# Four graph layers on one core: unread products in TensorE's idle time, a new order of layer 0, shorter neighbour lists, and a finish from two dot products

## The chip, the cores and the metric

The kernel runs on one core of one Trainium2 chip. A core has five engines with a queue each: TensorE (PE; its weight loads are shown as PEld), VectorE (DVE), ScalarE (ACT), GpSimd (POOL) and SyncE (SP), and DMA engines that move data between the chip's memory (HBM) and the on-chip memory (SBUF). Products land in PSUM[...]. The metric is the device time of one execution in microseconds. Before the change it is 1101.07 us (median of three runs, 1095.69 to 1104.53). The profiled execution, from which all times within the kernel come, took 1025.59 us, of which 1023.6 us lie between its first and last instruction.

## The reference

`x` has 4096 rows of 64 values and `adj` is a 4096 x 4096 matrix of zeros and ones, each one with a chance of 0.000976562, so about four neighbours per row. Four layers follow one another; each normalizes `x` per row, takes the positive part `h`, and adds its result to `x`. Layer 0 is the one that the change touches:

```python
c = 1.0 / r[0] ** 2
x_t = logmap0(x, c)
left = x_t @ w_att[:D, 0]
right = x_t @ w_att[D:, 0]
adj_att = jax.nn.sigmoid(left[:, None] + right[None, :] + b_att[0]) * adj
x_local = logmap(x[:, None, :], x[None, :, :], c)
support_t = jnp.einsum('ij,ijd->id', adj_att, x_local)
return proj(expmap(x, support_t, c), c)
```

So for each pair of neighbours it needs a hyperbolic logarithm (with square roots and logarithms), weights it with an attention value, sums over the neighbours, and maps the sum back. Layers 1 to 3 are products with `adj` (mean of neighbours, two hops with tanh, and a sum over the last 100 neighbours with halving weights).

## The kernel before, in words

Layer 0 (`neighbours`) uses that `adj` is almost empty. It has four kinds of work, for eight blocks of 512 rows:

- **The stream.** `load` brings the transposed adjacency in 64 pieces of 1 MB, three buffers in turn. ScalarE casts each to 8 bits (L781 into SBUF for the first three blocks, L784 and a store to HBM for the rest), for the later layers. TensorE multiplies it with `wpack` (L789), which packs 16 entries of a column into one number; after four pieces ScalarE adds a number that tells the word (`kt`, L795) and TensorE transposes into the key banks (L797).
- **The lists** (`lists`, on VectorE). For each of the 512 rows of a block the largest keys are taken (L819 to L821), taken apart into neighbour numbers (up to L858), and the first four neighbours per row go to `idx`. Rows with more put the rest into a common overflow list, which is packed over the partitions with two small products (`pb` L882, `pc` L903) and gives `ovx`, `own` and `rows_at`.
- **The gathers** (L941, on POOL): 24 indirect DMAs per block fetch rows of a table of 69 values per node (`rows_d`, written once at the beginning), 16 of them after `idx`, 8 after `ovx` and `own`. They land in `es` and `hi`, of which there are two, each for a pair of blocks. So the gathers of pair 2 wait for the product of pair 0, and those of pair 3 for that of pair 1.
- **The sums.** `chunk` forms inner products (L972 to L985), `weights` the weights of a pair of blocks with three ScalarE functions, each with a table load (L1009, L1016, L1032), L1063 scales the rows, `spots` makes the matrices that send overflow rows to their places (L1049), and TensorE sums in float32 (L1069, L1075) into the one bank `v`, from which ScalarE copies (L1080). `finish` (four groups of 8 x 128 rows) maps back and adds to `x` (L1100 to L1178).

The order is written by a planner at build time: it holds a clock, takes steps of these jobs by priority, and adds a cost for each (`yield 1.35`). The result is a fixed queue per engine. Its clock is VectorE's and POOL's alone:

```python
while any(queues.values()):
    now = clock["now"]
    while can_pack() and arrives(packed[0]) <= now + 1.0:
        pack_one()
    hungry = clock["pool"] - now < BACKLOG
    order = ["list", "chunk", "sum", "spot", "finish"] if hungry else ["chunk", "sum", "list", "spot", "finish"]
```

TensorE's and ScalarE's instructions are placed where the job that makes them happens to be recorded. Each engine then works through its queue from the front. Layers 1 to 3 (`layers123`) come behind layer 0 in every queue; most of their time is TensorE's (L1384, L1513, L1526, L1537).

Of the kernel before, what the change touches and what calls it, by code (L numbers as in the profile page):

```python
# [7 lines left out]
F32 = mybir.dt.float32  # L8
BF16 = mybir.dt.bfloat16
# [8 lines left out]
P = 128  # L18
# [32 lines left out]
HOLD, FETCH = -1.0, 1000.0  # L51
STREAM_AT, PACE_MB, PACKED = 7.0, 3.55, 5.0
ROWS_AT, PACE_DMA, LANDED, SUMMED, BACKLOG, SLOW = 46.0, 1.27, 5.0, 6.0, 20.0, 1.1
# [525 lines left out]
def neighbours(ctx, tc, x_in, x, sh, adj_t, adj8, a8, over):  # L579
# [20 lines left out]
    def load(b, v):  # L600
# [17 lines left out]
        noff, pattern=[[2 * N, LB], [0, 16]], base=1 - 127 * NCH, channel_multiplier=0,  # L618
        allow_small_or_imprecise_dtypes=True,
    )  # L620

# [8 lines left out]
    V.tensor_scalar(pr_i, pidx, 15, None, op0=ALU.bitwise_and)  # L630
    V.tensor_scalar(pc_i, pidx, 4, None, op0=ALU.logical_shift_right)
# [8 lines left out]
    V.tensor_scalar(pr_i, pidx, 7, 5, op0=ALU.bitwise_and, op1=ALU.logical_shift_left)  # L640
    V.tensor_scalar(pc_i, pidx, 3, None, op0=ALU.logical_shift_right)
# [3 lines left out]
    io128 = l0.tile([P, P], F32, name="io128")  # L645
    V.tensor_scalar_add(io128, io[:, :P], -1.0)
    before = l0.tile([P, P], BF16, name="before")
    V.tensor_scalar(before, sh.diff, 0.0, None, op0=ALU.is_gt)

# [19 lines left out]
    def inv_root(a, n, name):  # L669

        y = l0e.tile([P, n], F32, tag=f"ir_y{n}", name=f"{name}_y")
        e = l0e.tile([P, n], F32, tag=f"ir_e{n}", name=f"{name}_e")
        S.activation(y, a, AF.Abs_reciprocal_sqrt)
        yield 0.1
        V.tensor_mul(e, y, y)
        yield 0.2
        V.tensor_mul(e, e, a)
        yield 0.2
        V.scalar_tensor_tensor(e, e, -10.0 / 3.0, e, op0=ALU.add, op1=ALU.mult)
        yield 0.2  # L680
        V.scalar_tensor_tensor(y, e, 5.0, y, op0=ALU.add, op1=ALU.mult)
        yield 0.2
        V.tensor_scalar_mul(y, y, 0.375)
        yield 0.2
        return y
# [75 lines left out]

    def row_rest():

        V.tensor_scalar(beta, x2, negc_t, 1.0, op0=ALU.mult, op1=ALU.add)
        V.tensor_scalar_max(clipb, beta, MIN_NORM)


    keys = {}

    def pack(u):  # L770
# [3 lines left out]
        if part == 0:  # L774
            keys[b] = [psum.tile([P, 2, NW], F32, tag="k", bufs=4, name=f"keys{b}_{s}") for s in range(2)]
# [18 lines left out]
        kt = l0w.tile([P, 512], F32, tag="kt", name=f"kt{u}")  # L794
        S.activation(kt, pk, AF.Identity, bias=num[:, part : part + 1])  # L795
        for k in range(LB):
            T.transpose(  # L797
                keys[b][k // 2][:, k % 2, part * P : part * P + P], kt[:, k * P : (k + 1) * P], sh.ident
            )
        yield  # L800


    flags = l0.tile([P, NR, 4], F32, name="flags")
    V.memset(flags, 0.0)
# [4 lines left out]
    turned = [0]  # L809

    def lists(nb):
# [3 lines left out]
        k16 = tile_("k16", [LB, 16])  # L815
        scr = tile_("scr", [NW])
        for k in range(LB):
            kk = keys[nb][k // 2][:, k % 2, :]
# [5 lines left out]
        V.tensor_reduce(flags[:, nb, 0:1], k16[:, :, 15], AX.X, ALU.max)  # L824
        V.tensor_scalar(flags[:, nb, 0:1], flags[:, nb, 0:1], 256.0, None, op0=ALU.is_ge)
        yield 0.3


        ki, wi = tile_("ki", [LB, 16], I32), tile_("wi", [LB, 16], I32)
        wf, vf = tile_("wf", [LB, 16]), tile_("vf", [LB, 16])  # L830
        V.tensor_copy(ki, k16)
        V.tensor_scalar(wi, ki, NW - NCH, 4, op0=ALU.bitwise_and, op1=ALU.logical_shift_left)
        V.tensor_add(wf, wi, noff)
        yield 0.6
        V.tensor_scalar(wi, ki, NCH - 1, None, op0=ALU.bitwise_and)
        V.tensor_add(wf, wf, wi)
        V.tensor_scalar(wi, ki, 8, None, op0=ALU.logical_shift_right)
        V.tensor_copy(vf, wi)
        yield 0.8
        cand = tile_("cand", [LB, 3, 16])  # L840
        for lev in range(3):
            V.tensor_scalar(wi, vf.bitcast(I32), 0x7F800000, None, op0=ALU.bitwise_and)
            V.tensor_sub(vf, vf, wi.bitcast(F32))
            yield 0.4
            V.scalar_tensor_tensor(cand[:, :, lev, :], wi, NCH * 2.0**-23, wf, op0=ALU.mult, op1=ALU.add)
            V.scalar_tensor_tensor(cand[:, :, lev, :], wi, 0.0, cand[:, :, lev, :], op0=ALU.is_gt, op1=ALU.mult)
            yield 0.5
        V.tensor_reduce(flags[:, nb, 1:2], vf, AX.XY, ALU.max)

        j8 = tile_("j8", [LB, 8])  # L850
# [4 lines left out]
        ji = tile_("ji", [LB, NS], I32)  # L855
        V.tensor_copy(ji, j8[:, :, :NS])
        V.tensor_scalar(ji, ji, 2 * N - 1, None, op0=ALU.bitwise_and)
        V.tensor_scalar_min(idx[nb], ji, N)  # L858
        yield 0.6
        yield HOLD  # L860
        gather_slots(nb)
        yield FETCH + PACE_DMA * LB * NS
# [4 lines left out]
        yield 0.8  # L867
        ov, om = tile_("ov", [NV]), tile_("om", [NV])
# [7 lines left out]
        cnt, cnb, at0 = tile_("cnt", [1]), tile_("cnb", [1], BF16), tile_("at0", [1])  # L876
        mv = tile_("mv", [2 * NV + 2], BF16)
        V.tensor_scalar(om, ov, 0.0, None, op0=ALU.is_gt)
        V.tensor_reduce(cnt, om, AX.X, ALU.add)
        V.tensor_copy(cnb, cnt)  # L880
        pb = psum.tile([P, 512], F32, tag="s", bufs=1, name=f"pb{nb}")
        T.matmul(pb[:, :1], before, cnb, start=True, stop=True)  # L882
        V.tensor_copy(mv[:, :NV], ov)
        V.tensor_sub(mv[:, NV : 2 * NV], ov, mv[:, :NV])
        V.tensor_copy(mv[:, 2 * NV + 1 :], p_f)
        V.tensor_copy(flags[:, nb, 2:3], ov[:, NV - 1 : NV])
        yield 1.5

        bi, end = tile_("bi", [1], I32), tile_("end", [1])
        from_, mine = tile_("from", [512], BF16), tile_("mine", [512], BF16)  # L890
        V.tensor_copy(at0, pb[:, :1])
        V.tensor_scalar(from_, io, at0, None, op0=ALU.is_gt)
        V.tensor_add(end, at0, cnt)
        V.scalar_tensor_tensor(mine, io, end, from_, op0=ALU.is_le, op1=ALU.mult)
        yield 1.4
        V.tensor_copy(bi, at0)
        V.tensor_scalar(bi, bi, P - 1, None, op0=ALU.bitwise_and)
        V.tensor_copy(mv[:, 2 * NV : 2 * NV + 1], bi)
        V.tensor_scalar(flags[:, nb, 3:4], end, float(NO * P), 0.0, op0=ALU.subtract, op1=ALU.max)
        pc = psum.tile([P, 512], F32, tag="s", bufs=1, name=f"pc{nb}")  # L900
        pe = pc[:, : NO * (2 * NV + 2)].rearrange("p (c e) -> p c e", c=NO)
        for c in range(NO):
            T.matmul(pe[:, c, :], mine[:, c * P : (c + 1) * P], mv, start=True, stop=True, skip_group_check=True)  # L903
        yield 0.7

        got, ei, ti = tile_("got", [NO, 2]), tile_("ei", [NO], I32), tile_("ti", [NO], I32)
        tf, ef, rw = tile_("tf", [NO]), tile_("ef", [NO]), rows_at[nb]
        its, num2 = tile_("its", [NO, NV]), tile_("num2", [NO, 2, NV])
        V.tensor_copy(got, pe[:, :, 2 * NV :])
        V.tensor_scalar(ti, got[:, :, 0], -1.0, p_f, op0=ALU.mult, op1=ALU.add)  # L910
        V.tensor_scalar(ti, ti, P - 1, None, op0=ALU.bitwise_and)
        V.tensor_copy(tf, ti)
        yield 0.7
        V.tensor_tensor(its, io128[:, None, :NV].to_broadcast([P, NO, NV]), bc(tf, NV), op=ALU.is_equal)
        V.tensor_mul(
            num2, pe[:, :, : 2 * NV].rearrange("p c (t s) -> p c t s", t=2),
            its[:, :, None, :].to_broadcast([P, NO, 2, NV]),
        )
        V.tensor_reduce(tf, num2, AX.XY, ALU.add)
        V.tensor_copy(ei, tf)  # L920
        yield 1.3
        V.tensor_scalar(ti, ei, 2 * N - 1, None, op0=ALU.bitwise_and)
        V.tensor_scalar_min(ovx[nb], ti, N)
        V.tensor_scalar(ti, ei, 13, None, op0=ALU.logical_shift_right)
        V.tensor_scalar(ef, tf, 0.0, None, op0=ALU.is_gt)
        V.scalar_tensor_tensor(rw, got[:, :, 1], float(NCH), ti, op0=ALU.mult, op1=ALU.add)
        V.scalar_tensor_tensor(rw, rw, float(1 + LB * nb), ef, op0=ALU.add, op1=ALU.mult)
        V.tensor_scalar_min(own[nb], rw, float(N))
        yield 1.3
        gather_packed(nb)  # L930
        yield FETCH + PACE_DMA * 2 * NO
        V.scalar_tensor_tensor(rw, ti, float(P), got[:, :, 1], op0=ALU.mult, op1=ALU.add)
        V.scalar_tensor_tensor(rw, rw, 1.0, ef, op0=ALU.add, op1=ALU.mult)
        yield 0.4
# [53 lines left out]
    def weights(se, e_g, x2i, lf, name):  # L988
# [23 lines left out]
        yield 0.6  # L1012

# [3 lines left out]
        yield 0.2  # L1017
        V.tensor_mul(e, y, y)
# [15 lines left out]
        yield 0.2  # L1034
        V.scalar_tensor_tensor(den, den, -1.0, gap, op0=ALU.add, op1=ALU.subtract)
# [7 lines left out]
    vs, spot = {}, {}  # L1043
# [7 lines left out]

    def sums(g, q0, q1):
# [5 lines left out]
        if q0 == 0:  # L1058
            vs[g] = l0w.tile([P, 8, DQ], F32, tag="vs", bufs=4, name=f"vs{g}")
        for q in range(q0, q1):  # L1060
# [4 lines left out]
            bank = psum.tile([P, 512], F32, tag="v", bufs=1, name=f"v{nb}")  # L1065
            pv = bank[:, : LB * DQ]
            slots = es[g][:, q, : LB * NS, :DQ].rearrange("p (k s) e -> p s k e", k=LB)
            for s in range(NS):
                T.matmul(  # L1069
                    pv.rearrange("p (k e) -> p k e", k=LB), sh.ident, slots[:, s], start=(s == 0), stop=False,  # L1070
                    skip_group_check=True,
                )
            for c in range(NO):
                for k in range(LB):
                    T.matmul(  # L1075
# [603 lines left out]
```

## Time and profile before

| | value |
|---|---|
| time, median of 3 | 1101.07 us |
| profiled span | 1023.6 us |
| last adjacency piece packed | from 256.6 us |
| gathers on POOL | 192, from 61.3 to 349.2 us |
| end of layer 0 (last addition to `x`) | 440.1 us |
| first large product of layer 1 | 491.2 us |
| mean granted TensorE clock | 0.807 |

The span in 40 slices of 25.6 us: each digit is the busy share of a slice in tenths, PEclk the granted TensorE clock in tenths of full speed, DMA the share of the DMA engines. The first 17 slices are layer 0.

```profile
PE   3545556555622630017999989998996899999996
DVE  4769775769278548864455531113444345444443
ACT  4666574555301231222111111112222343434342
POOL 0347777676067500000000000000000000000000
PEclk9955559555565765557899999998998899999999
DMA  8699997999011100072000000000000000000000
```

And the groups of gathers, pack products and block sums: line, engine, operation, output and inputs, count, then busy us and mean ns of one, and the idle time of the engine before them with what ended it.

```profile
L789 PE MATMUL pk<-a,wpack 128*128 128x512 bf16 x256 | 111.3, 582 | 97.4 <-DMA a<-in_adj_t 97.4
L941 POOL DMA_INDIRECT es<-rows_d,idx x128 | 128.1, 1001 | 95.3 <-issue 35.0
L1069 PE MATMUL v<-es,ident 128*128 128x260 f32 x64 | 25.8, 571 | 30.1 <-issue 23.1
L1075 PE MATMUL v<-es,spot 128*128 128x65 f32 x256 | 37.8, 318 | 0.0
```

[...] several in a row take less than count times mean.

### The profile page before, as it was taken

The page shows a single profiled execution, that of the slowest core. Times are in us where ns is not written, and L with a number is a line of the kernel's source. Part 1 is how long each engine was busy: PE and PEld are TensorE (multiplying, and loading weights), DVE is VectorE, ACT ScalarE, POOL GpSimd, SP SyncE. Part 2 cuts the span into 40 slices and gives each one's busy share as a digit, 9 for nine tenths or more (in the row PEclk, how much of TensorE's full clock was granted, in tenths as well). Part 3 has the DMA queues.
Part 4 walks back from the last instruction along what each step waited for, and adds up shares of the span by engine and source line. Part 5 has one row for each costly group of instructions (what it writes and reads, how often), then busy time and mean ns, then how long its engine had stood idle before and what let it go on. Part 6 is the DMA issues. An engine that isn't in the chain of part 4 may idle for free.

```text
span 1023.6 us, 14344 instructions
## 1 busy us (share of the span) xinstructions
PE 705.4 (69%) x5602; PEld 532.8 (52%) x5602; DVE 551.8 (54%) x1705; ACT 344.2 (34%) x465; POOL 200.5 (20%) x208
## 2 busy tenths in 40 slices
PE   3545556555622630017999989998996899999996
PEld 1112115211512530017899989998995565656564
DVE  4769775769278548864455531113444345444443
ACT  4666574555301231222111111112222343434342
POOL 0347777676067500000000000000000000000000
PEclk9955559555565765557899999998998899999999
DMA  8699997999011100072000000000000000000000
GB/s 284 235 355 332 373 377 250 379 378 360 13 21 28 19 0 0 0 316 96 1 1 1 2 1 2 1 1 2 2 2 1 1 1 12 1 11 1 11 2 14
DMA packets 49248, 99.49 MB, mean 97 GB/s; under 512 B 6802, under 2 KB 6802, under 8 KB 48274
## 3 DMA queue, kind: packets, MB, share of 16 engines
q1 hardware_dynamic: 35232, 79.70, 21.5%
q10 hardware_dynamic: 7794, 11.98, 3.2%
q0 software_dynamic: 6144, 6.80, 3.1%
q8 instruction: 46, 0.75, 0.3%
q14 instruction: 32, 0.26, 0.1%
HBM read 85.79 MB, written 12.67 MB: 96 GB/s over the span
## 4 chain that ended last, share of the span: by engine, by line
PE 49%; DVE 5%; ACT 3%; issue 1%; ACTq 0%
PE l2b_acc L1384 9%; PE l2a_acc L1384 9%; PE l_acc L1513 8%; PE l_acc L1384 8%; PE cnt L1537 7%; PE cnt L1526 5%; PE l_u L1344 1%; PE l_t L1331 1%; ACT l_h L1333 1%; DVE l_agg L1365 1%; PE l2b_u L1344 0%; PE l_u L1338 0%; DVE l_r L1351 0%; DVE ln_c L1609 0%; DVE ln_c L1615 0%
## 5 line engine op out<-in xcount | busy, mean ns | idle before, releaser
L1384 PEld LDWEIGHTS <-a 128*128 128x128 fp8e4 x3072 | 265.5, 99 | 9.3 <-issue 6.9
L789 PE MATMUL pk<-a,wpack 128*128 128x512 bf16 x256 | 111.3, 582 | 97.4 <-DMA a<-in_adj_t 97.4
L1533 DVE TENSOR_SCALAR wt<-cnt 128x512 int16<-128x512 f32 x128 | 88.5, 692 | 121.0 <-PE cnt L1526 121.0
L941 POOL DMA_INDIRECT es<-rows_d,idx x128 | 128.1, 1001 | 95.3 <-issue 35.0
L1534 ACT ACTIVATE wt<-cnt,low_t 128x512 int16<-128x512 f32 x128 | 87.9, 687 | 134.8 <-PE cnt L1526 134.8
L789 PEld LDWEIGHTS <-wpack 128*128 128x128 bf16 x256 | 33.0, 130 | 159.3 <-issue 144.9
L1513 PE MATMUL l_acc<-y_b,wt 128*128 128x192 bf16 x1024 | 106.7, 247 | 0.0
L1513 PEld LDWEIGHTS <-wt 128*128 128x128 bf16 x1024 | 89.1, 98 | 31.3 <-issue 1.7
L1537 PE MATMUL cnt<-a,fill 128*128 128x512 fp8e4 x248 | 81.2, 382 | 20.3 <-DVE wt L1533 20.0
L1384 PE MATMUL l_acc<-y_a,a 128*128 128x193 bf16 x1024 | 94.9, 253 | 0.0
L784 ACT CAST f<-a 128x2048 fp8e4<-128x2048 f32 x40 | 75.9, 1898 | 48.2 <-DMA a<-in_adj_t 47.1
L1384 PE MATMUL l2b_acc<-y_a,a 128*128 128x192 bf16 x1024 | 89.2, 249 | 3.0 <-DVE y_a L1353 3.0
L1384 PE MATMUL l2a_acc<-y_b,a 128*128 128x192 bf16 x1024 | 88.1, 248 | 3.0 <-DVE y_b L1353 3.0
L1526 PE MATMUL cnt<-a,tri 128*128 128x512 fp8e4 x256 | 77.2, 383 | 0.0
L781 ACT CAST a<-a 128x2048 fp8e4<-128x2048 f32 x24 | 45.3, 1894 | 22.9 <-DMA a<-in_adj_t 18.5
L1069 PE MATMUL v<-es,ident 128*128 128x260 f32 x64 | 25.8, 571 | 30.1 <-issue 23.1
L1526 PEld LDWEIGHTS <-tri 128*128 128x128 bf16 x256 | 24.7, 97 | 37.4 <-issue 22.4
L1639 PE MATMUL po<-one,over 128*1 128x1 f32 x2 | 0.2, 163 | 58.8 <-DVE over L1281 58.8
L1075 PEld LDWEIGHTS v<-es,spot 128*128 128x128 f32 x256 | 38.8, 238 | 1.2
L1537 PEld LDWEIGHTS <-fill 128*128 128x128 bf16 x248 | 24.0, 97 | 28.1 <-issue 21.3
L1075 PE MATMUL v<-es,spot 128*128 128x65 f32 x256 | 37.8, 318 | 0.0
L1365 DVE TENSOR_REDUCE l2a_agg<-l2a_acc 128x128 f32<-128x384 f32 x16 | 8.9, 558 | 51.4 <-PE l2a_acc L1384 51.4
(336 smaller groups left out, 828.6 us busy)
## 6 DMA issues: line engine op xcount, KB each, us to landing
a<-in_adj_t SPq DMA_DIRECT2D x64, 1024.0 KB, 8.3
adj<-f ACTq DMA_DIRECT2D x40, 256.0 KB, 6.4
a<-adj SPq DMA_DIRECT2D x5, 2048.0 KB, 19.5
es<-rows_d,idx POOLq DMA_INDIRECT x128, 5.5
rows_d<-tab ACTq DMA_DIRECT2D x1, 1104.0 KB, 4.8
x<-in_x SPq DMA_DIRECT2D x1, 1024.0 KB
out<-z SPq DMA_DIRECT2D x4, 256.0 KB, 2.1
es<-rows_d,ovx POOLq DMA_INDIRECT x32, 5.4
```

The lines of the kernel that those rows point to most:

```text
L781: S.copy(a8[b][:, 4 * at : 4 * at + 4, :], a, saturate=False)
L784: S.copy(f8, a, saturate=False)
L789: T.matmul(pk, wflat[:, w * P : (w + 1) * P], bits[:, j, :, 1], start=(w == 0), stop=(w == 15),)
L941: G.indirect_dma_start(out=dst, out_offset=None, in_=rows_d, in_offset=bass.IndirectOffsetOnAxis(ap=at, axis=0))
L1069: T.matmul(pv.rearrange("p (k e) -> p k e", k=LB), sh.ident, slots[:, s], start=(s == 0), stop=False, skip_group_check=True,)
L1075: T.matmul(pv[:, k * DQ : (k + 1) * DQ], spot[nb][:, c, k * P : (k + 1) * P], es[g][:, q, LB * NS + c, :DQ], start=False, stop=(c == NO - ...
L1384: T.matmul(acc, a8[n // 4][:, c, n % 4 * P : (n % 4 + 1) * P], y3[:, c, :cols], start=(c == first[0] and k % 2 == 0), stop=(c == last[-1] ...
L1513: T.matmul(accs[k // 2][:, k % 2, : 3 * D], wts[k // 4][:, (k % 4) * P : (k % 4 + 1) * P].bitcast(BF16), y3[:, c, : 3 * D], start=(c == NC ...
L1526: T.matmul(cnt[b], tri, masks[b], start=head_, stop=last, skip_group_check=True)
L1533: V.tensor_scalar(wts[0], cnt[0], -(128.0 - MAX_NEIGH) * UNIT, 0.0, op0=ALU.add, op1=ALU.max)
L1534: S.activation(wts[1], cnt[1], AF.Relu, bias=low_t)
L1537: T.matmul(cnt[b], fill, masks[b], start=False, stop=False, skip_group_check=True)
```

## The change

It concerns layer 0 alone.

- Unread products (`fill`): TensorE multiplies constants into a PSUM bank that nobody reads, where the planner's clock of TensorE runs out of work, 780 times in all. They are to keep TensorE's clock up.
- An order that follows all engines: the planner now holds clocks for TensorE and ScalarE too. A job that needs an answer of theirs says so (`yield "ACT", 1.6`) and is not continued before. The products of a sum are put out in pieces, and the copy out of PSUM is placed behind them. There are two `v` banks.
- Keys copied to SBUF (`bring`): two ScalarE copies per block, so that two key banks are enough instead of four; these banks are used for the second `v` and for `fill`.
- Shorter lists: the keys are coded in another way, so that fewer VectorE instructions take them apart, and the overflow flags are gathered once at the end (`overflow`).
- Finish from two dot products: `dots` forms h.v and v.v for each group; everything else in `finish` is computed on one number per row, for three groups at once and for the last one, and only the final combination touches all 64 columns again.

The diff, cut:

```diff
-STREAM_AT, PACE_MB, PACKED = 7.0, 3.55, 5.0
-ROWS_AT, PACE_DMA, LANDED, SUMMED, BACKLOG, SLOW = 46.0, 1.27, 5.0, 6.0, 20.0, 1.1
+STREAM_AT, PACE_MB = 8.0, 3.5
+ROWS_AT, PACE_DMA, LANDED, BACKLOG, SLOW, AHEAD = 46.0, 1.25, 3.0, 12.0, 1.05, 0.6
...
-        if part == 0:
-            keys[b] = [psum.tile([P, 2, NW], F32, tag="k", bufs=4, name=f"keys{b}_{s}") for s in range(2)]
+        if part == 0:
+            banks[b] = [psum.tile([P, 2, NW], F32, tag="k", bufs=2, name=f"keys{b}_{s}") for s in range(2)]
...
+    def bring():
+
+        if later and turned[0] >= later[0] - 1:
+            b = later.pop()
+            keys[b] = l0w.tile([P, LB, NW], F32, tag="keys", name=f"keyt{b}")
+            for s in range(2):
+                S.copy(keys[b][:, 2 * s : 2 * s + 2, :], banks[b][s])
...
-            V.scalar_tensor_tensor(cand[:, :, lev, :], wi, NCH * 2.0**-23, wf, op0=ALU.mult, op1=ALU.add)
-            V.scalar_tensor_tensor(cand[:, :, lev, :], wi, 0.0, cand[:, :, lev, :], op0=ALU.is_gt, op1=ALU.mult)
+            V.scalar_tensor_tensor(cand[:, :, lev, :], wi, 256 * 2.0**-23, wf, op0=ALU.mult, op1=ALU.add)
...
+    fill_t = psum.tile([P, 512], F32, tag="fill", name="fill_t")
+    fill_in = io.bitcast(BF16)[:, :512]
+
+    def fill(n):
+
+        for _ in range(n):
+            T.matmul(fill_t, wflat[:, :P], fill_in, start=True, stop=True, skip_group_check=True)
...
-            bank = psum.tile([P, 512], F32, tag="v", bufs=1, name=f"v{nb}")
+            bank = psum.tile([P, 512], F32, tag="v", bufs=2, name=f"v{nb}")
             pv = bank[:, : LB * DQ]
...
+            pieces.append(products(nb, pv))
+            taken.append((q, pv))
+        yield "PIECES", 0.0
+        for q, pv in taken:
+            n = (2 * g + q) * LB
+            S.copy(vs[:, n : n + LB, :], pv.rearrange("p (k e) -> p k e", k=LB))
+        yield "ACT", 0.8
+
+    def dots(g):
+
+        rows = slice(g * 8, g * 8 + 8)
+        t, sq = block(f"d_t{g}"), block(f"d_s{g}")
+        S.activation(sq, vs[:, rows, :D], AF.Square)
+        V.tensor_mul(t, h[:, rows, :], vs[:, rows, :D])
+        yield 0.7
+        V.tensor_reduce(hv[:, rows], t, AX.X, ALU.add)
+        yield 0.7
+        V.tensor_reduce(vv[:, rows], sq, AX.X, ALU.add)
+        yield 0.7
...
+        def pack_one():
+            m = packed[0]
+            next(units[m // 4])
+            if m % 8 != 7:
+                bring()
+            at = arrives(m)
+            clock["ACT"] = max(clock["ACT"], at) + (2.9 if m % 4 == 3 else 2.2)
+            clock["PE"] = max(clock["PE"], at) + (1.9 if m % 4 == 3 else 1.1)
+            packed[0] += 1
+            if m < 10:
+                fill(9)
+                clock["PE"] += 2.0
...
-                queues["finish"].append(Job("finish", nb, finish(g, 0, 8), after(("sum", nb))))
+                queues["dots"].append(Job("dots", g, dots(g), after(("sum", nb))))
+        for g0, g1 in ((0, NQ - 1), (NQ - 1, NQ)):
+            queues["finish"].append(Job("finish", g0, finish(g0, g1), after(*[("dots", g) for g in range(g0, g1)])))
...
+            if clock["PE"] <= now + AHEAD:
+                if not pieces:
+                    fill(2)
+                    clock["PE"] = max(clock["PE"], now) + 0.44
+                    continue
+                try:
+                    clock["PE"] = max(clock["PE"], now) + next(pieces[0])
+                except StopIteration:
+                    pieces.pop(0)
+                    if not pieces:
+                        job = queues["sum"][0]
+                        job.until, job.pieces = clock["PE"] + 0.3, False
+                continue
```

## The prediction

> **What bounds the kernel now.** I first cut the span into stretches, to see which engine fills which stage. The columns are the stretch, then busy us (instructions) of PE, PEld, DVE, ACT and POOL, the granted TensorE clock, the DMA share and GB/s.
>
> ```profile
> 60.00:252.00 192.00, 111.06 (x362) 47.11 (x363) 142.38 (x572) 111.42 (x92) 140.85 (x144) 0.60 1.01 352
> 252.00:286.00 34.00, 22.83 (x92) 18.15 (x92) 11.03 (x35) 9.63 (x11) 0.00 (x0) 0.55 0.12 44
> 286.00:350.00 64.00, 15.09 (x94) 13.45 (x94) 50.72 (x194) 11.51 (x25) 49.12 (x48) 0.64 0.17 27
> 350.00:391.00 41.00, 17.74 (x79) 16.00 (x77) 21.68 (x82) 10.86 (x20) 0.00 (x0) 0.58 0.01 1
> 391.00:440.00 49.00, 0.00 (x0) 0.00 (x0) 43.42 (x173) 11.47 (x18) 0.00 (x0) 0.50 0.00 0
> ```
>
> Layer 0 ends at 440 us. Until 257 us the adjacency stream fills the DMA engines (share 1.01). Then come 180 us in which no engine is full: first POOL stands still while TensorE works at half clock, then POOL gathers again, and from 350 to 440 VectorE is alone. From 491 to the end TensorE is busy 489 of 533 us at clock 0.97; the change leaves those layers alone, so the prediction is about layer 0.
>
> Next the waits of layer 0 (engine line waited for: us in total, times, longest).
>
> ```profile
> ACT vs L1080 <- PE v L1075: 71.8, 7, 14.4
> PE pb L882 <- DVE cnb L880: 35.3, 2, 26.0
> POOL es L941 <- PE v L1075: 34.9, 1, 34.9
> ACT w L1009 <- DVE w L1008: 29.7, 2, 26.1
> DVE at L891 <- PE pb L882: 26.1, 5, 10.5
> DVE spot L1049 <- PE v L1075: 15.9, 2, 9.2
> ```
>
> Each is an engine held at the head of its queue. The third costs most: POOL issued its 144th gather at 250.6 us and had to wait until 286.5 us, because the next one overwrites rows of the second pair of blocks, whose product was not done. The timeline of TensorE says why that came so late, and what its clock costs.
>
> ```profile
> 165.54 1.92 PE L1069 MATMUL v<-es,ident 128*128 128x260 f32 x8
> 167.30 3.68 PE L1075 MATMUL v<-es,spot 128*128 128x65 f32 x32
> ...
> 267.25 3.83 PE L1069 MATMUL v<-es,ident 128*128 128x260 f32 x8 [6.44 <-DVE es L1063]
> 270.87 6.93 PE L1075 MATMUL v<-es,spot 128*128 128x65 f32 x32
> ```
>
> One block's sum takes 5.6 us (1.92 + 3.68) on a warm TensorE and 10.8 us (3.83 + 6.93) on a cold one. At 267 us TensorE waits for VectorE, which lost 6.4 us at 256 us to the ScalarE (casts and three table loads ahead of its answer). VectorE then lost 9.2 and 6.7 us waiting for the cold products to release the spot matrices.
>
> [...] The two pairs of lines agree: a factor of 2.0 and 1.9, and the fast pair follows 10 us of dense work. [...] The trace shows 1.28 us and the activation 1.29 us after the load's start, so I use 1.3.
>
> **The change part by part.**
>
> *Unread products.* 780 matmuls of 512 bf16 columns, in TensorE's queue wherever the plan sees it idle. Warm, four pack products take 1.06 us with 512 columns each, so one is at most 0.27 us; cold, 0.465 (1.86 / 4). 432 of them stand ahead of the last pack product: 432 x 0.27 = 117 us, beside 256 x 0.27 = 68 us of pack products, inside the 245 us from the first load to the last. They are hidden in waits for loads. Behind them in the queue wait the small pb and pc products, for which VectorE waits, but the plan puts only about 0.6 us ahead. In exchange each sum costs 5.6 instead of up to 10.8 us. Seven sums stand in the waits; in the tail the last one counts in full: 5 us. Lower bound 0 (the clock stays cold), and a loss if it does: see the third rival.
>
> *Keys copied to SBUF.* Two ScalarE copies per block; nearest row: the kt activation, 0.69 us for the same 512 columns out of PSUM. 8 x 1.4 = 11 us on an engine busy 111 of 192 us, hidden except for the first block, where VectorE has nothing else. There ScalarE is blocked until the table's store is issued (49.6 us), then casts 1.9 us, then copies 1.4: VectorE begins at about 53. The VectorE maxima gain nothing: 418 ns from PSUM, 428 ns from SBUF.
>
> *Shorter lists.* Counted in the built order: 10 fewer small instructions up to the first gather, 12 behind it, per block. Spacing in the trace is about 0.2 us: 4.4 us per block, 35 us of VectorE over eight. While the stream lasts they are beside it; ahead of the first gather 2.2 us are on the path, so it starts at 53 + 5.3 (maxima) + 4.2 = 62.5 instead of 61.3 us.
>
> *The order.* The product of the second pair now stands ahead of the seventh block's list; before, it stood behind it. So does each product relative to the gathers that reuse its rows. That should remove POOL's 34.9 us. Then POOL itself is the bound: 192 gathers at 1.25 us (0.94 busy + 0.30 issue) are 240 us, so the last is issued no earlier than 302.5, against 349 now. The price is that TensorE's queue mixes list products and loads tightly: a load that lands later than planned holds VectorE. The plan reckons with 3.5 us per load; undisturbed the trace shows 3.6 (73.8 to 153.4, 22 loads), later 3.8 (180.0 to 256.7, 20 loads). The last load lands at 153.4 + 25 x 3.75 = 247, where the plan has 232. VectorE is then some 13 us behind the plan; the gathers, which start 6 late, have about 10 us of backlog. I take 5 us of new POOL idle, bounds 0 and 20.
>
> *Finish.* Before, four groups of 16.2 us each (391.37 to 407.58), three and a half of them after the last sum. After, each group has three large VectorE operations in the dot products and four at the end instead of twelve of 0.6 to 0.7 us; three groups share one run of small ones and can lie in the waits for the last gathers. Left at the end: 16.2 - 5 x 0.66 + 6 x 0.17 = 13.9 us for the last group.
>
> *Sum.* Last gather issued 302.5 + 5 = 307.5; landing 5.5 (the median) = 313. Chunk, weights and scaling of the last block took 10.2 us (363.1 to 373.3); some 45 small operations of the merged finish now lie between, 45 x 0.17 = 8 us, part of them in ScalarE's waits: take 6. So 329. Product 5.6, copy 0.6, dot products and finish 13.9, one exposed table load 1.3, and some unnamed waiting, 2: 352.6. Layer 0 ends 87 us earlier. The head of layer 1 (440 to 491) is a chain of layernorms through three engines; a warm clock saves 1 us there once. 1101 - 87 - 1 = 1013 us. (The timed runs lie 75 us above the profiled one; I take that as unchanged. Were it proportional, the saving would be 6 us larger.)
>
> **The rivals.**
>
> 1. *The plan slips as the old one did.* If late loads in TensorE's queue hold VectorE again and again, POOL idles 20 to 45 us more. For it: the old order lost a comparable amount in exactly such waits. Against it: the clock, the two product banks and the copies placed later each take one of them away. Layer 0 would end at 372 to 397, the time be 1033 to 1058; middle 1045.
> 2. *Finish does not overlap.* POOL's gap closes, but the merged finish falls behind the last sum, where VectorE is already full: 50 small operations (8.5 us) and twelve large ones (8.4), of which 6 us are reckoned with above: 1013 + 11 = 1024. Against it: in the built order its small operations stand ahead of the last product, and only the twelve large ones around it.
> 3. *TensorE becomes the bound, slower.* If the clock does not rise, 432 x 0.465 = 201 us of unread products join 119 us of pack products and 18 of transposes: 338 us from 12 on, the stream ends at 350 instead of 257, and with some 100 us of tail layer 0 ends at 450 to 455. 1113 us. Against it: between 150 and 175 us, the one early stretch in which TensorE was dense, the granted clock was 0.86.
>
> **How the numbers follow.** Forecast 1013: 0.66. First rival 0.18, second 0.10, third 0.06. Better than forecast by no POOL idle and a proportional offset: 1013 - 5 - 6 - a few = 995; a little below that I set the low end, 986. The high end, 1050, takes in the second rival and half of the first. Faster by over 1% are all but the third and the worst of the first: 0.93. Within 1%: 0.02. Slower: 0.05.
>
> **What the profile would show.** Right: clock near 1.0 throughout layer 0; POOL's gathers at 1.25 us with gaps below 10 us in all, the last near 305; the fp32 products at 1.9 and 3.7 us; last load near 247; one short finish at the end, layer 0 over near 352. Wrong: gathers that wait for a product or a list, VectorE waiting for pb or pc behind a load, a stream that ends after 260 us, or a clock below 0.9. Layers 1 to 3 differing by more than 3 us would overthrow the assumption that they are untouched.

## The result, and the profile after

The changed kernel takes 1031.19 us (median of 4, 1028.23 to 1036.35), the kernel before 1101.25 us; the ratio is 0.9374, 95% interval 0.932 to 0.9427. The forecast was 1013. So 70 us are gone where 88 were expected; the direction and most of the size are right, the share of the parts is not, as the runs below show.

One thing has to be said before the profiles can be compared. The first profile of before, on which the prediction rests, was of an execution 75 us shorter than the timed ones; profiled again (run before_again) the same kernel has a span of 1095.2 us. That is the profile to set beside the one of after, whose span is 1029.7 us. First their slices (25.7 us each after, 27.4 us before_again): of after the granted clock, the DMA share and POOL.

```profile
PEclk9988898798788869976899999998998899999999
DMA  8687598798693110063000000000000000000000
POOL 0345654664626750000000000000000000000000
```

And of before, profiled again:

```profile
DMA  8697797399911100003500000000000000000000
POOL 0355675265706740000000000000000000000000
```

In the first profile of before the DMA row read 9 in seven of the eight slices from the third to the tenth. Here both rows are torn: the stream of the adjacency stands still again and again. The five stretches that were shown of before, now of after (busy us of PE, PEld, DVE, ACT, POOL, then clock, DMA share, GB/s):

```profile
60.00:252.00 192.00, 130.59 (x587) 64.32 (x599) 98.88 (x365) 93.98 (x87) 110.32 (x114) 0.83 0.81 267
252.00:286.00 34.00, 19.72 (x72) 7.37 (x71) 15.08 (x59) 14.16 (x13) 21.29 (x23) 0.74 0.68 216
286.00:350.00 64.00, 55.02 (x274) 31.08 (x280) 44.33 (x164) 25.92 (x36) 34.54 (x35) 0.90 0.55 181
350.00:391.00 41.00, 29.55 (x131) 21.96 (x132) 22.40 (x79) 8.77 (x13) 21.36 (x21) 0.67 0.14 20
391.00:440.00 49.00, 48.74 (x255) 27.64 (x258) 33.60 (x142) 11.29 (x22) 0.00 (x0) 1.00 0.00 1
```

The stream's share is 0.81 instead of 1.01 and it still runs after 286 us; POOL no longer stops at 252, but it made only 114 gathers by then. The waits show what stopped it. Of after, the first 445 us:

```profile
DVE from L910 <- remote: 51.3, 5, 13.2
POOL es L962 <- DVE rw L935: 50.5, 7, 15.4
ACT kt L814 <- remote: 34.9, 5, 10.7
POOL es L962 <- PE v L1097: 4.5, 1, 4.5
```

And of the queue that issues the adjacency loads (SyncE), in the same stretch of after:

```profile
SPq L602 <- PE pk L808: 107.6, 35, 12.6
SPq L602 <- remote: 91.4, 11, 16.6
```

Of before, profiled again, the first 520 us:

```profile
POOL es L941 <- PE v L1075: 33.8, 1, 33.8
POOL es L941 <- DVE ef L925: 30.5, 2, 20.0
ACT kt L795 <- remote: 21.7, 2, 12.0
```

The 34 us for the second pair's product are 4.5 now; POOL waits for packed lists instead (`rw`), whose VectorE steps wait for TensorE's `pb` (L910). "remote" means that the wait ended without a signal that the profile can tie to a finished instruction. The loads themselves wait so for 91 us in after (63 us in before_again, none in the first profile of before), and the stream stands still meanwhile. This is what such a wait looks like in the timeline of after:

```profile
72.56 0.36 PE L901 MATMUL pb<-cnt,upto 128*128 128x1 f32 x2
73.68 1.46 PE L1083 MATMUL fill_t<-io,wpack 128*128 128x512 bf16 x6
78.47 0.49 DVE L910 TENSOR_SCALAR from<-io,pb 128x512 bf16<-128x512 f32 x1 [13.20 <-remote]
```

`pb` is done at 72.92 us and TensorE goes on to its fills, but VectorE, which waits for `pb` alone, starts at 78.47. The signal stands in the trace 5.5 us behind the recorded end of `pb`; the rest of the 13.2 us is ordinary waiting. Waits that end so, with their ordinary part, sum to 142 us over the computing engines between 60 and 400 us in after, to 72 us in before_again, and to 0 in the first profile of before. Where no signal was late, as in the first profile of before, each one lies within 0.02 us of the recorded end of its instruction; that here the signal is late, and not the recorded end too early, is a reading of that and was not shown by itself.

Milestones in us. The last column is the changed kernel without the last of its unread products (run fill_stop), in whose trace no signal is late; the forecast belongs beside it. The first product with `adj` of layer 1 starts at 464.8 us in the first profile of before; the 491.2 us given at the beginning is where the first long run of them starts.

| | before, first profile | before_again | after | fill_stop | forecast |
|---|---|---|---|---|---|
| last pack product ends | 258.5 | 310.8 | 317.3 | 260.5 | 247 (last load) |
| last gather issued | 348.3 | 407.6 | 376.7 | 315.7 | 307.5 |
| last block sum ends | 381.5 | 451.5 | 423.6 | 348.6 | 334.6 |
| layer 0 ends | 440.1 | 510.0 | 437.5 | 362.5 | 352.6 |
| first product with `adj` of layer 1 | 464.8 | 534.7 | 470.0 | 387.1 | |
| from there to the end | 558.8 | 560.5 | 559.7 | 557.7 | unchanged |

### The profile page after: what moved, and what is told of

Its sections match the earlier page's. It is cut to its first block, busy times and chain, and to the rows that moved or that the text cites. A ratio compares the mean times of both kernels' runs of the same rounds, so it can differ in the third digit from the quotient of the medians.

```text
span 1029.7 us, 15753 instructions
## 1 busy us (share of the span) xinstructions
PE 843.4 (82%) x6411; PEld 602.2 (58%) x6438; DVE 495.2 (48%) x1451; ACT 344.2 (33%) x471; POOL 198.3 (19%) x210
## 4 chain that ended last, share of the span: by engine, by line
PE 61%; DVE 15%; another core or an unknown queue 8%; ACT 6%; issue 5%; DMA 4%; ACTq 0%; DVEq 0%; SPq 0%
PE l2b_acc L1481 9%; PE l2a_acc L1481 9%; PE l_acc L1610 8%; PE l_acc L1481 8%; PE cnt L1634 7%; PE fill_t L1083 6%; PE cnt L1623 5%; DMA a<-in_adj_t 3%; PE v L1097 3%; PE v L1090 1%; PE l_u L1441 1%; PE pk L808 1%; ACT f L803 1%; DVE scr L854 1%
## 5 line engine op out<-in xcount | busy, mean ns | idle before, releaser
L1083 PE MATMUL fill_t<-io,wpack 128*128 128x512 bf16 x761 | 194.1, 405 | 11.0 <-issue 10.4
L1083 PEld LDWEIGHTS <-wpack 128*128 128x128 bf16 x780 | 80.6, 104 | 110.0 <-issue 32.1
L808 PE MATMUL pk<-a,wpack 128*128 128x512 bf16 x248 | 77.8, 434 | 28.7 <-DMA a<-in_adj_t 23.7
L808 PEld LDWEIGHTS <-wpack 128*128 128x128 bf16 x256 | 27.0, 107 | 66.9 <-issue 34.9
L818 PE MATMUL keys<-ident,kt 128*128 128x128 f32 x64 | 14.1, 358 | 49.6 <-ACT kt L814 41.4
L800 ACT CAST a<-a 128x2048 fp8e4<-128x2048 f32 x24 | 45.4, 1895 | 21.5 <-DMA a<-in_adj_t 14.4
L1097 PE MATMUL v<-es,spot 128*128 128x65 f32 x256 | 35.6, 295 | 9.5 <-issue 9.4
L818 PEld LDWEIGHTS keys<-ident,kt 128*128 128x128 f32 x64 | 8.8, 175 | 59.1 <-ACT kt L814 48.8
L1097 PEld LDWEIGHTS v<-es,spot 128*128 128x128 f32 x256 | 35.8, 215 | 11.5 <-issue 10.1
```

Source lines behind the costliest of these rows:

```text
L800: S.copy(a8[b][:, 4 * at : 4 * at + 4, :], a, saturate=False)
L808: T.matmul(pk, wflat[:, w * P : (w + 1) * P], bits[:, j, :, 1], start=(w == 0), stop=(w == 15),)
L1083: T.matmul(fill_t, wflat[:, :P], fill_in, start=True, stop=True, skip_group_check=True)
L1097: T.matmul(pv[:, k * DQ : (k + 1) * DQ], spot[nb][:, c, k * P : (k + 1) * P], es[g][:, q, LB * NS + c, :DQ], start=False, stop=(c == NO - ...
```

## The experiments

The kernels were timed in three sets, each beside before and each on another chip: before_again to pace_385, old_finish to plain_rows, and the last four. In the first two sets before takes 1094 to 1096 us; in the third it takes 1021.5 us, and none of the four traces shows a late signal. So kernels of different sets are compared by their ratios to before, or by stretches of their traces. A trace is of one execution.

**before_again.** The kernel before, unchanged.

> The kernel before, unchanged, profiled once more, because its first profile (1025.6 us) lies 75 us below its timed runs. Theory A: the first profile was of an unusual execution; another one shows about 1100 us, layer 0 ends near 515 instead of 440 us, and the 75 us stand as waits in the stream (last piece packed near 330 instead of 257 us). Theory B: profiling itself makes this kernel quicker; then the profile is near 1025 us again and only the timed runs are near 1100.

1092.88 us (ratio 0.998, 0.994 to 1.002); the profile's span is 1095.2 us, its last pack product ends at 310.8. Theory A: profiling does not make it quicker, the first profile was unlike the timed runs.

**no_fill.** All 780 unread products left out, everything else in the same order.

```diff
-        for _ in range(n):
+        for _ in range(0):
             T.matmul(fill_t, wflat[:, :P], fill_in, start=True, stop=True, skip_group_check=True)
```

> The changed kernel without its unread products, all other instructions in the same order. The kernel leaves out only work that nobody reads. Theory 1 (the fills are worth the tail's warm sums, some 5 us, and a few us of warm list products): 1036 to 1045 us, the stream as late as with them (325 us), granted clock near 0.8. Theory 2 (the fills crowd TensorE's queue, and the late answers to VectorE, ScalarE and the loads come from them): 960 to 1010 us, the stream ends before 270 us and the waits named remote are gone. Theory 3 (without them everything in layer 0 runs at half clock and the plan slips): 1060 us or more.

1006.73 us (ratio 0.9205, 0.9134 to 0.9276): 24 us less than with them by the times, of two sets, and 19 us by the ratios; the two intervals are apart. In the traces layer 1's first product starts 24.0 us earlier (446.1 against 470.0). Theory 2 has the sign, but not the mechanism: the stream still ends at 306.7 us, waits named remote still sum to 99 us, and the mean clock is 0.813 instead of 0.904. The clock was bought and did not pay.

**fill_tail.** Only those behind the last pack product.

```diff
-        for _ in range(n):
+        for _ in range(n if packed[0] == 8 * NR else 0):
```

> Unread products only behind the last pack product (348 of 780). Theory 1 (their worth is in the tail's warm sums): same as with all of them, 1025 to 1036 us. Theory 2 (those among the pack products delay the stream): 960 to 1005 us. Theory 3 (those among the pack products keep the list products and the sums warm): 1045 us or more, near the kernel without any.

1018.77 us (0.9301, 0.9232 to 0.9371). Its middle lies between the two, as if about half of the loss belonged to the products in the stream and half to those in the tail, but its interval overlaps both of theirs. None of the three theories had that.

**pace_385.** The plan with a truer pace of the loads.

```diff
-STREAM_AT, PACE_MB = 8.0, 3.5
+STREAM_AT, PACE_MB = 8.0, 3.85
```

> The changed kernel, its plan reckoning with 3.85 instead of 3.5 us per load, so that lists and sums stand behind fewer pack products and more unread products fill the gaps. Theory 1 (late loads at the head of TensorE's queue hold VectorE and POOL): POOL's waits for the packed list shrink from 50 us to below 30, 1000 to 1020 us. Theory 2 (something else stalls the stream, and the order follows it): 1025 to 1045 us, with the same waits. Theory 3 (the order now puts the stream itself later): above 1045 us.

1028.57 us (0.9392, 0.9315 to 0.9468), the same as after; POOL's waits for the packed list are 46.0 us instead of 50.5. Theory 2: the plan's pace is not what costs.

**old_finish.** From here the base is no_fill. Dot products and merged finish replaced by the old finish of four groups.

```diff
-                queues["dots"].append(Job("dots", g, dots(g), after(("sum", nb))))
-        for g0, g1 in ((0, NQ - 1), (NQ - 1, NQ)):
-            queues["finish"].append(Job("finish", g0, finish(g0, g1), after(*[("dots", g) for g in range(g0, g1)])))
+                queues["finish"].append(Job("finish", nb, finish(g, 0, 8), after(("sum", nb))))
```

> The kernel without unread products, with the finish of before (twelve large VectorE operations and its own run of small ones for each of the four groups) in the place of the dot products and the merged finish. Theory 1 (the finish is half of the gain; the tail from the last sum to layer 1 took 83 us before and 39 now): 1042 to 1054 us against 1007, the tail near 80 us. Theory 2 (the new order hides three of the four groups in the waits for gathers, whatever their form): 1010 to 1025 us, the tail below 60 us.

1004.37 us (0.9216, 0.9124 to 0.9307): no difference, which is less than even theory 2 expected. From the last sum to the end of layer 0 it takes 26.2 us (no_fill 13.9, before 58.6): the order hides most of the old finish. The 12 us more there are not seen in the time: in its trace the last sum ended 14 us earlier (393.2 against 407.5). Why is open.

**old_order.** The planner of before, with new lists, key copies and finish.

```diff
-            if clock["PE"] <= now + AHEAD:
-                if not pieces:
-                    fill(2)
...
+            hungry = clock["FETCH"] - now < BACKLOG
+            rest = ["spot", "dots", "finish", "over"]
+            order = (["list", "chunk", "sum"] if hungry else ["chunk", "sum", "list"]) + rest
...
+                    elif kind == "PIECES":
+                        while pieces:
+                            drain(pieces.pop(0))
```

> The kernel without unread products, its instructions placed by the planner of before (clocks of VectorE and POOL alone, products at once where the scaled rows are recorded, the old priorities and constants); lists, key copies and finish stay new. Theory 1 (the order closes POOL's gap, some 35 to 40 us between first and last gather): 1035 to 1050 us against 1007. Theory 2 (shorter lists and the second bank carry it, and late signals from TensorE blur any order): 1000 to 1018 us. Theory 3 (the new order is the worse one under late signals): below 1000 us.

1035.01 us (0.9485, 0.9405 to 0.9565): theory 1, though the order is worth 28 us (31 by the ratios), not 35 to 40. The last gather is issued at 385.8 instead of 367.9 us. But POOL's wait for the second pair's product is absent under the old planner too, so that gap is not what the order closes. (One constant of the old planner, `PACKED`, was set to 6.5 instead of 5.0.)

**long_lists.** 22 idle small VectorE instructions more per block, 10 of them ahead of the first gather.

```diff
+        def more(n):
+            for _ in range(n):
+                V.tensor_scalar_add(spare, noff, 1.0)
```

> The kernel without unread products, with 22 idle small VectorE instructions more per block (10 ahead of its first gather, 12 behind), as many as the lists lost; nobody reads their result. Theory 1 (the lists' length is hidden while the stream lasts): 1005 to 1013 us against 1007. Theory 2 (VectorE's work per list is on the path of gathers that wait for lists): 8 x 4.4 us = 35 us, most of it seen, 1028 to 1042 us.

1011.98 us (0.9266, 0.9188 to 0.9344) against 0.9205 (0.9134 to 0.9276). Theory 1: of 35 us of VectorE work some 5 to 7 are seen by the medians. The intervals overlap and allow anything from nothing to about 18 us, but not 35.

**plain_rows.** Indirect gathers replaced by plain DMAs of the same size from the same queue.

```diff
-        G.indirect_dma_start(
-            out=dst, out_offset=None, in_=rows_d, in_offset=bass.IndirectOffsetOnAxis(ap=at, axis=0)
-        )
+        G.tensor_copy(seen, at)
+        G.dma_start(dst, rows_d[1 : P + 1, :])
```

> The kernel without unread products, with each indirect gather replaced by a plain DMA of the same size and from the same queue that reads fixed rows, behind a small POOL copy of the index, so that the sums are over the wrong rows. It is to tell where the late signals of TensorE, VectorE and ScalarE (updates seen up to 28 us after the end of their instruction, from 66 us to 370 us) come from. Theory 1 (from the indirect gathers): no update more than 0.4 us late, the stream ends near 258 instead of 307 us, the time below 960 us. Theory 2 (from the busy stream itself): late updates as before, stream near 300 us, 985 us or more.

932.46 us (0.8525, 0.8436 to 0.8615; two executions only, 929.3 and 935.6), no wait named remote, no signal late, last pack product at 252.5 us. Theory 1: the late signals come with the indirect form. The plain form also reads the same 128 rows each time where the indirect one reads scattered rows; which of the two matters this run doesn't separate.

**lists_only.** Old planner, old finish, no unread products; lists, key copies and the second `v` bank are left of the change (edits: those of old_order and old_finish together).

> Without unread products, with the planner of before and the finish of before: what is left of the change is the shorter lists, the keys in SBUF and the second bank for sums. Theory 1 (order and finish each hide the same tail, so that without both the whole tail of some 80 us is back): 1065 to 1080 us; the gathers end near 386 us as with the new finish in the old order. Theory 2 (lists and keys are worth little, the finish alone made the old order better): 1088 to 1097 us. Theory 3 (the finish is worth nothing in either order): 1030 to 1042 us.

1006.78 us where before takes 1021.51 (0.9863, 0.9826 to 0.990): 15 us less (10 to 18), which is what lists, copies and bank are worth together beside the old order and finish. Scaled by the ratio to a before of 1096 this is 1081 us, at the edge of theory 1, and its reason holds in the main: from the last sum to layer 1's first product it takes 65 us (before 83, old_order 43, no_fill 39), so most of the tail is back. The last gather is issued at 328.2 us; the 386 of theory 1 was a figure with late signals.

**fill_stop.** The changed kernel without the 92 unread products behind the last sum.

```diff
                 if not pieces:
-                    fill(2)
+                    fill(2 if queues["sum"] else 0)
```

> The changed kernel without the 92 last of its unread products, which stand behind the last sum's copy; the other 688 and the order stay. Theory 1 (they hold layer 1: its first VectorE instruction, a cast into memory that the unread products' operands occupied, waits 7.7 us for the last of them): 1021 to 1026 us against 1031. Theory 2 (they keep TensorE warm for the head of layer 1 and cost nothing): 1030 to 1036 us.

949.34 us (0.9299, 0.9264 to 0.9334) where before takes 1021.51. The numbers expected were for a before of 1101; after's own ratio is 0.9374 (0.932 to 0.9427), so by time alone the two are not told apart. The trace decides: from the end of layer 0 to layer 1's first product it takes 24.6 us, in after 32.6, in no_fill and before 24.7. Theory 1 for these 7.9 us; the lines of this trace are shown below. Against lists_only, of the same set, the new order and finish together are worth 57 us here, in spite of the other 688 unread products.

**after_plain.** The changed kernel, all unread products, plain DMAs (edit as in plain_rows).

> The changed kernel with its unread products, each indirect gather replaced by a plain DMA of fixed rows behind a small POOL copy of the index (so the sums are over the wrong rows): no signal comes late then. Theory 1 (the unread products hurt only by what queues behind late signals, and by the tail's 8 us): 932 us of the kernel without them, less 5 us for warm sums, plus 8: 930 to 940 us. Theory 2 (they delay the stream in any case): 945 us or more. Theory 3 (they are worth what was forecast, and more): 925 us or less.

951.61 us (0.9315, 0.9281 to 0.9348), no late signal. Without unread products it was 932.46 (plain_rows, of another set): theory 2. In the traces layer 1's first product starts 21.2 us later (393.5 against 372.2). They cost even where every signal is in time.

**before_plain.** The kernel before with plain DMAs.

> The kernel before with each indirect gather replaced by a plain DMA of fixed rows behind a small POOL copy of the index (sums over the wrong rows): its stages without late signals. Theory 1 (late signals cost both kernels about 70 us, so the forecast from the undisturbed profile holds for the difference): 1010 to 1030 us, last pack near 258 us. Theory 2 (the order of before suffers more from them than the new one): 1000 us or less.

1016.88 us (0.9969, 0.9944 to 0.9995): inside theory 1's range, last pack product at 257.8 us. But in this set before itself takes 1021.51 us, about as long as in its first profile (1025.59), where no signal was late, so the run doesn't tell what they cost before; its two profiles do (layer 0 ends at 440.1 and 510.0). Here plain DMAs save 5 us; where signals come late they saved no_fill 74.

## Why the prediction was right in the main, and which step failed

*Layers 1 to 3 untouched.* Right: 559.7 us from layer 1's first product, 560.5 before.

*The 75 us between timed and profiled runs, taken as unchanged.* Right in size, and now it is known where it lies: in the late signals. Without them layer 0 goes from 440.1 to 362.5 us (fill_stop); with them from 510.0 to 437.5. The kernels lose 70 and 75 us, and the difference, which the forecast needs, is nearly the same: 77.5 and 72.6. That was luck as much as argument; nothing in the first profile hinted at it.

*Unread products: gain 5 us.* This is the step that failed, in sign. They cost about 20 us: 24 by the times (1031 against 1007), 19 by the ratios, 21 in the two traces without late signals. The gain was too large from the start: it sets 5.6 us against the 10.8 us of the sum at 267 us, but the last block's sum of before, the one that counts in the tail, took 8.1 us in the same profile (373.38 to 381.50):

```profile
373.38 3.81 PE L1069 MATMUL v<-es,ident 128*128 128x260 f32 x8 [13.77 <-issue]
376.98 4.52 PE L1075 MATMUL v<-es,spot 128*128 128x65 f32 x32
```

That products which nobody reads would raise the clock was an estimate; the mean clock is 0.904 with them (after) and 0.813 without (no_fill). The cost was put at nothing. "Hidden in waits for loads" was true for their sum and false for each: in the traces TensorE works its queue in order (the product of the last block in fill_stop could start at 339.20 us and starts at 343.20, behind the fills), so a filler is free only if it ends before the next useful instruction could start. The plan places fillers by its own clock, and whenever VectorE is quicker than the plan, the product it has made ready stands behind them. Here the last block in fill_stop: VectorE's scaling, the fills, the product.

```profile
329.17 14.19 PE L1083 MATMUL fill_t<-io,wpack 128*128 128x512 bf16 x64
337.69 1.51 DVE L1114 TENSOR_TENSOR es<-es,w 128x1300 f32<-128x1300 f32 x1
343.20 1.92 PE L1090 MATMUL v<-es,ident 128*128 128x260 f32 x8
```

The same block in no_fill:

```profile
398.36 1.51 DVE L1114 TENSOR_TENSOR es<-es,w 128x1300 f32<-128x1300 f32 x1
399.98 2.50 PE L1090 MATMUL v<-es,ident 128*128 128x260 f32 x5 [10.20 <-issue]
```

Scaled at 339.20, multiplied at 343.20, with no idle time of TensorE between: 4.0 us behind the last of 64 fills, against 0.1 us without them; in after, fill_tail and after_plain it is 4.0 us too. For the block before it the wait is 5.8 us in fill_stop and 7.4 in after, and again 0.1 in no_fill. And in after's tail, behind the last copy:

```profile
423.62 21.53 PE L1083 MATMUL fill_t<-io,wpack 128*128 128x512 bf16 x98
445.19 0.23 DVE L1408 CAST idb<-ident 128x128 bf16<-128x128 f32 x1 [7.73 <-PE fill_t L1083]
```

The finish took 13.9 us and the fills 21.5; layer 1's first VectorE instruction waits 7.73 us for them (that it waits is shown; that it does so because it writes memory which their operands held was not tried). In the stream it is the same, with cold products. After the wait for the load at 59 us, after_plain has

```profile
62.55 3.62 PE L1084 MATMUL fill_t<-io,wpack 128*128 128x512 bf16 x8
65.97 1.48 PE L808 MATMUL pk<-a,wpack 128*128 128x512 bf16 x4
67.29 2.75 PE L1084 MATMUL fill_t<-io,wpack 128*128 128x512 bf16 x12
69.87 1.06 PE L808 MATMUL pk<-a,wpack 128*128 128x512 bf16 x4
```

and plain_rows, without fills, starts the same two groups of pack products here:

```profile
63.34 1.87 PE L808 MATMUL pk<-a,wpack 128*128 128x512 bf16 x4 [0.49 <-DMA a<-in_adj_t]
66.01 1.86 PE L808 MATMUL pk<-a,wpack 128*128 128x512 bf16 x4 [0.80 <-DMA a<-in_adj_t]
```

The first eight fills run at half clock: they take 3.62 us, in after too, where the granted clock is 0.50 from 58 to 66 us and eight later ones (from 95.68 us, clock 1.00) take 1.89. Ahead of them, up to 59 us, TensorE had nothing to do for 6.5 us. The pack products start 2.6 and 3.9 us later, and the next three loads are issued 2.2 to 3.3 us later. The lag grows and shrinks along the stream; the last of the 64 loads is issued 6.7 us later (248.9 against 242.2).

The sum, after against no_fill: last gather 8.9 us later (376.7, 367.9); from there to the end of the seventh block's scaling 0.9; from that to the end of the last sum 32.3 us instead of 26.1, although its two sums are shorter; from layer 0 to layer 1 7.9. Together 23.9. The pair without late signals (after_plain against plain_rows) gives 7.7, -0.4, 6.1 and 7.9. The warm sums did save something: the last took 5.4 us against 7.6 in no_fill, the one before it 5.4 against 8.2. That is half of the 5 us forecast for one, and these four places gave back several times as much.

*Keys copy.* First gather forecast 62.5, measured 62.1. Right for copy and shorter list together; the copy alone was not tried.

*Shorter lists, mostly hidden.* Not contradicted (long_lists). Lists, copies and second bank together are worth 15 us (lists_only).

*The order.* The forecast of 307.5 us for the last gather is 8 us too early where signals are in time (315.7). POOL's 34.9 us gap is gone, but the credit was wrong: under the old planner, with new lists, key copies and second bank, there is no such wait either (old_order, lists_only). Which of these three closes it was not tried. The order is still worth 28 us, between the gathers and in the tail. The plan's pace of 3.5 us, which the prediction blamed for a lag of VectorE, was not the cause of the slips (pace_385).

*Finish: 13.9 us left at the end.* The equal number is a coincidence: the forecast's stretch from the last sum to the end of layer 0 has 18.0 us (copy, table load and unnamed waiting beside the 13.9), and measured is 13.9 for all of it (423.6 to 437.5). With the last gather 8.2 us later than forecast, 5.8 us more from there to the last sum (where the fills cost 6) and these 4.1 us less, fill_stop's layer 0 ends 9.9 us after the forecast. And the 16.2 us groups of the old form would not have stood there 3.5 times: with the new order they leave 26.2 us (old_finish), with the old planner and the new lists 38.8 (lists_only), in before 58.6. Order and finish each remove most of the same tail, so their gains can't be added. What the new form is worth beside the new order stays open: 12 us in the tail of the trace, nothing in the time.

*Rivals.* The first, more POOL idle, describes after's profile (waits for packed lists, 50.5 us), but the cause is late signals, which before has too; without them the wait is 2.9 us (fill_stop). The second did not occur. The third had the right culprit, unread products in TensorE's queue, and the wrong size: the clock did rise (0.67 to 1.00 in the five stretches where it was 0.50 to 0.64), and they cost about 20 us, not 100. Most of the signs named for a wrong prediction did appear in after (a stream that ends at 317 us, gathers that wait for lists, VectorE that waits for `pb`, a clock below 0.9 in three of the stretches); the late end of the stream is before's too, once it was profiled again (310.8).

Why 1031 and not 1013: the unread products missed by 24 to 29 us (5 gained in the forecast, 19 to 24 lost as measured). The rest of the change did 4 to 11 us better than forecast: 1007 as timed, 1014 by its ratio, against 1018. So the total came close in part because two errors point in opposite directions. Two smaller misreadings of the first profile change no sum: two table loads (1.28 us each), not three, stand ahead of ScalarE's answer at 262.7 us, and between the dense work and the fast pair at 165.5 us lies an idle time of 2.5 us.

## What to carry to other kernels

Filler work in an in-order queue is free only if it is over before the next useful instruction is ready: place it by an event, keep it short, and stop it ahead of the last use, for a plan that is slower than the chip turned filler into a wait here, of 4.0 us at the last sum and 7.7 us at the end. A clock that rises is no gain by itself: here its mean rose from 0.813 to 0.904 and the kernel lost 19 to 24 us. Ask which instruction on the path gets shorter, and by how much. And before working from a profile, compare its span with the timed runs: here they differed by 75 us, nearly all of it in layer 0 (70 us between the two profiles).

## What the runs showed of the hardware

While indirect gathers run on POOL (62 to 378 us in after), signals of TensorE, VectorE and ScalarE came up to 28.4, 18.7 and 16.2 us after the end of their instruction (28.4 for a pack product that ends at 255.33 us): each instruction that sends a signal was set beside the next signal of its engine in the trace, and where signals are late several come at once, as one record. Of the instructions that ended before the first gather, or more than 2 us after the last was issued, none was late, in any of the eight traces that have late signals, and none at all in plain_rows, where 192 plain DMAs of the same size stand in the same queue. But none was late either in three executions with indirect gathers (the first profile of before, fill_stop, lists_only). So in these runs the indirect form (or its scattered rows) was needed for it and did not suffice. What else is needed the runs don't tell: two of those three traces come from the third set, on a chip where even before took 1021.5 us in the middle, so the chip or its state is a rival that was not varied on its own. Layer 0 loses some 70 us by it (no_fill 1006.7 against plain_rows 932.5, in two sets; layer 0 of before 440.1 against 510.0), as much as the change brings.
